# Two attention layers on eight images: the key sums' product delayed and two sums of seven given to GpSimd, layer norm taken out of ScalarE's queue, group norm between projections, opening reordered

## The chip, the core and the metric

One core of a Trainium2 chip. The metric is the device time of one execution in microseconds (us).

## The reference, cut to what matters

```python
# x: (8, 512, 32, 32) float32: 8 images (batches), 512 channels, 1024 positions
# layer 0: layer norm over channels, 8 heads of 64, projection, residual
xn = layer_norm(x_flat)
q, k, v = xn @ Wq.T + bq, xn @ Wk.T + bk, xn @ Wv.T + bv       # split in 8 heads
attn = softmax(q k^T / 8)                                        # per head, 1024 x 1024
x1 = (attn v) @ Wo.T + bo + x_flat
# layer 1: group norm (32 groups), one head of 512, projection, residual
h = group_norm(x1)
out = x1 + wp (softmax((wq h)^T (wk h) / sqrt(512)) (wv h)) + bp
```

Everything is float32.

## The kernel before

Channels lie on the partitions, four tiles of 128 x 1024 per image. Two heads (a *pair*) fill 128 partitions. A pair sees 512 query positions, so an image has 8 pairs, each worked in two *groups* of four key blocks (m = 0 to 3, then 4 to 7): 16 groups, i = 0 to 15. Softmax needs no maximum here; a check of the denominators (`junk`) guards that. The denominators come in two steps: VectorE adds up a pair's eight tiles of exponentials (the *key sums*, seven additions), and TensorE multiplies the result by ones (their *product*, `den`). To *evict* a result is to read it out of its bank of PSUM, the memory that TensorE writes, so that the bank comes free.

TensorE's order is fixed by the program. For the other engines the framework orders the queue, mostly but not always as the program gives the work: in batch 1 of this kernel GpSimd adds `x` for the mean at 640.78 us, ahead of the second pair's `o` at 657.86, which the program gives first. So orders are read from the traces below, and an edit can move more than its own lines.

```python
big  = tc.tile_pool(bufs=33)              # 128 x 1024 tiles in SBUF
ps_s = tc.tile_pool(bufs=3, space=PSUM)   # wide_psum: scores, projections, mean, variance
ps_a = tc.tile_pool(bufs=2, space=PSUM)   # bank: acc, den, group norm

class Pair:
    def scores(self, ms):                  # one group
        for m in ms:
            s = wide_psum(...)             # two matmuls into it
            p = big_tile(...)
            nc.scalar.activation(p, s, AF.Exp, scale=...)
            self.p[m] = p
            if m == 1:   self.sum = big_tile(...); nc.vector.tensor_add(self.sum, self.p[0], p)
            elif m > 1:  nc.vector.tensor_add(self.sum, self.sum, p)
    def values(self, ms): ...              # matmuls into self.acc, a bank
    def end(self):
        den = bank(...)                    # key sums' product: ones x self.sum
        o = half_tile(...);  nc.scalar.copy(o, self.acc)
        nc.vector.reciprocal(rden, den)
        check_sums(den, rden)              # junk: VectorE's last reader of den's bank
        nc.gpsimd.tensor_mul(o, o, rden)

def layer_norm_mean(b, xt):
    # x sums: three tensor_add on gpsimd; mean = ones_c x sum on TensorE
    for c in range(NC): nc.vector.tensor_sub(xt[c], xt[c], mean)
    # squares: activation(Square) on scalar, three tensor_add on gpsimd

def layer_norm_scale(b, xt, sq):
    # variance on TensorE, sqrt on scalar
    nc.vector.reciprocal(rstd, rstd)       # 128 x 1024
    for c in range(NC):
        nc.gpsimd.tensor_mul(xt[c], xt[c], rstd)
        nc.vector.tensor_scalar(xt[c], xt[c], g0, be0, ALU.mult, ALU.add)

for i, (p, ms) in enumerate(groups):       # one image
    groups[i + 1][0].scores(groups[i + 1][1])
    p.values(ms)
    if ms[-1] == NM - 1: os.append(p.end())
    if i == 3: sq = layer_norm_mean(b + 1, x_next)         # of the next image
    if i == 7: h_next = layer_norm_scale(b + 1, x_next, sq)
    if i == 9: project_out(b, 0, os[:NC], x1, stats)       # psx, then x1 = psx + bias + x
# then: two k projections of the next image, project_out of the other half,
# two k projections, group norm, layer 1
# [cuts: weight products, q/k/v projections, group norm, layer 1]
```

Of the kernel before, what the change touches and what calls it, by code (L numbers as in the profile page):

```python
# [16 lines left out]
P = 128  # L17
# [28 lines left out]
def fast_path(ctx: ExitStack, tc: tile.TileContext, x: bass.AP, vecs: dict, weights: dict, out: bass.AP,  # L46
# [46 lines left out]
    x_next = load_x(0)  # L93

# [9 lines left out]
    def load_w(pool, n):  # L104
        t = pool.tile([P, NC, C], F32, tag=f"w_{n}", name=f"w_{n}")
        nc.scalar.dma_start(out=t, in_=weights[n].rearrange("(c p) o -> p c o", p=P))
        return t

    def load_chunks(n):

        chunks = []
        for g in range(NC // 2):
            t = big_tile(f"w_{n}_{g}")
            nc.scalar.dma_start(out=t.rearrange("p (c o) -> p c o", o=C),
                                in_=weights[n][ts(g, 2 * P), :].rearrange("(c p) o -> p c o", p=P))
            chunks += [t[:, ts(k, C)] for k in range(2)]
        return chunks

# [22 lines left out]
    def weight_products():  # L141
        def natural(t, n):

            chunks = []
            for g in range(NC // 2):
                ps = wide_psum(f"pst_{n}_{g}")
                for k in range(2):
                    oc = 2 * g + k
                    for c in range(NC):
                        nc.tensor.transpose(ps[:, k * C + c * P : k * C + (c + 1) * P], t[c][:, ts(oc, P)], ident)  # L150
                r = big_tile(f"nat_{n}_{g}")
                nc.vector.tensor_copy(r, ps)
                chunks.append(r)
            return [chunks[oc // 2][:, ts(oc % 2, C)] for oc in range(NC)]

        def product(dst, lhs, rhs, n):
            for g in range(NC // 2):
                ps = wide_psum(f"psw_{n}_{g}")
                for k in range(2):
                    for oc in range(NC):  # L160
                        nc.tensor.matmul(ps[:, ts(k, C)], lhs[oc][:, ts(2 * g + k, P)], rhs(oc),
                                         start=(oc == 0), stop=(oc == NC - 1))
                nc.scalar.copy(dst[:, 2 * g : 2 * g + 2, :].rearrange("p a c -> p (a c)"), ps)

        wq, wk, wv, wp = (load_chunks(n) for n in ("q1", "k1", "v1", "p1"))
        for n in ("k0", "v0", "q0", "o0"):
            w[n] = load_w(const, n)
        nc.scalar.dma_start(out=bv0_row, in_=vecs["bv0"].rearrange("(a c) -> a c", a=1).to_broadcast((P, C)))
        nc.scalar.dma_start(out=bm_row, in_=vecs["bp1"].rearrange("(a c) -> a c", a=1).to_broadcast((P, C)))
        nq, nk = natural(wq, "q1"), natural(wk, "k1")  # L170
        product(wa, nq, lambda oc: nk[oc], "a")
        ps = bank("psu")
        for c in range(NC):
            for oc in range(NC):
                nc.tensor.matmul(ps[:, c : c + 1], nk[oc][:, ts(c, P)], vec("bq1", oc),
                                 start=(oc == 0), stop=(oc == NC - 1))
        nc.vector.tensor_copy(ua, ps[:, :NC])
        nv = natural(wv, "v1")
        product(wm, nv, lambda oc: wp[oc], "m")
        ps = bank("psb")  # L180
        for oc in range(NC):
            nc.tensor.matmul(ps, vec("bv1", oc).to_broadcast((P, P)), wp[oc],
                             start=(oc == 0), stop=(oc == NC - 1))
        nc.vector.tensor_add(bm_row, bm_row, ps)


    def layer_norm_mean(b, xt):

        t = [big_tile(f"lns_{b}_{i}") for i in range(2)]
        for i in range(2):  # L190
            nc.gpsimd.tensor_add(t[i], xt[2 * i], xt[2 * i + 1])
        nc.gpsimd.tensor_add(t[0], t[0], t[1])
        mean = wide_psum(f"mean_{b}")
        for hf in range(NH):
            nc.tensor.matmul(mean[:, ts(hf, HB)], ones_c, t[0][:, ts(hf, HB)], start=True, stop=True)
        for c in range(NC):
            nc.vector.tensor_sub(xt[c], xt[c], mean)
        sq = [big_tile(f"sq_{b}_{i}") for i in range(2)]
        nc.scalar.activation(sq[0], xt[0], AF.Square)
        for c in range(1, NC):  # L200
            nc.scalar.activation(sq[1], xt[c], AF.Square)
            nc.gpsimd.tensor_add(sq[0], sq[0], sq[1])
        return sq

    def layer_norm_scale(b, xt, sq):
# [5 lines left out]
        nc.vector.reciprocal(rstd, rstd)  # L211
        for c in range(NC):
            nc.gpsimd.tensor_mul(xt[c], xt[c], rstd)
            nc.vector.tensor_scalar(xt[c], xt[c], vec("g0", c), vec("be0", c), ALU.mult, ALU.add)  # L214
        return xt

    def group_norm(b, xt, stats):
# [10 lines left out]
        nc.vector.tensor_add(dev, dev, mv[:, :, 1])  # L228
        pv = bank(f"pv_{b}")
        nc.tensor.matmul(pv[:, :NC], grp, dev, start=True, stop=True)  # L230
        sc = small.tile([P, NC], F32, tag="gsc", name=f"gsc_{b}")
# [17 lines left out]

    def project(tag, wt, bias, ht, ocs, engine):  # L250

        res = []
        for oc in ocs:
            r = big_tile(f"{tag}_{oc}")
            ps = wide_psum(f"ps{tag}_{oc}")
            for hf in range(NH):
                for c in range(NC):
                    nc.tensor.matmul(ps[:, ts(hf, HB)], wt[:, c, ts(oc, P)], ht[c][:, ts(hf, HB)],  # L258
                                     start=(c == 0), stop=(c == NC - 1))
            if engine == "act":  # L260
                nc.scalar.activation(r, ps, AF.Identity, bias=bias(oc))  # L261
            else:
                nc.vector.tensor_scalar(r, ps, bias(oc), None, ALU.add)
            res.append(r)
# [24 lines left out]
    class Pair:  # L289
# [9 lines left out]
        def scores(self, ms):  # L299
            c, q = self.c, ts(self.hf, HB)  # L300
            for m in ms:
# [11 lines left out]
                elif m > 1:  # L313
                    nc.vector.tensor_add(self.sum, self.sum, p)  # L314

        def values(self, ms):
            if self.acc is None:
                self.acc = bank(f"acc_{self.tag}")
            for m in ms:
                for i in range(2):  # L320
                    col = self.c * P + i * D
                    nc.tensor.matmul(self.acc[i * D : (i + 1) * D, :], self.vts[m][:, col : col + D],  # L322
                                     self.p[m][:, ts(i, HB)], start=(m == 0), stop=(m == NM - 1))

        def end(self):
# [4 lines left out]
            o = half_tile(f"o_{self.tag}")  # L330
            nc.scalar.copy(o, self.acc)
# [68 lines left out]
    def head_of(b, ht):  # L400

        q = project(f"q{b}", w["q0"], lambda oc: vec("bq0", oc), ht, range(NC), "act")
        return q

    with tc.manual_schedule(engines={PE}):
        sq = layer_norm_mean(0, x_next)
        weight_products()
        ht = layer_norm_scale(0, x_next, sq)
        kt = project("k0", w["k0"], lambda oc: vec("bk0", oc), ht, range(NC), "dve")
        vts = project_v("v0", w["v0"], bv0_row, ht)  # L410
        qt = project("q0", w["q0"], lambda oc: vec("bq0", oc), ht, range(NC), "act")
        for b in range(B):
# [5 lines left out]
            os = []  # L418
            x_next = load_x(b + 1) if more else None
            groups[0][0].scores(groups[0][1])  # L420
            for i, (p, ms) in enumerate(groups):
# [3 lines left out]
                if ms[-1] == NM - 1:  # L425
                    os.append(p.end())
                if i == 3 and more:
                    sq = layer_norm_mean(b + 1, x_next)
                if i == 7 and more:
                    h_next = layer_norm_scale(b + 1, x_next, sq)  # L430
                if i == 9:
                    project_out(b, 0, os[:NC], x1, stats)
            if more:
                kn = project(f"k{b + 1}", w["k0"], lambda oc: vec("bk0", oc), h_next, (0, 1), "dve")
            project_out(b, 1, os[NC:], x1, stats)
            if more:
                kn += project(f"k{b + 1}", w["k0"], lambda oc: vec("bk0", oc), h_next, (2, 3), "act")
# [403 lines left out]
```

## Time and profile before

| | |
|---|---|
| time, median of the three first runs | 3566.05 us (3565.84 to 3566.79) |
| span of the profile | 3563.5 us |
| TensorE busy | 3344.0 us |
| first scores of heads | at 181.4 us |
| period of a batch, start of heads to start of heads | about 435 us (1 to 7), 339.3 for the last, which prepares no next image |

TensorE is the bound by its busy time. The prediction below shows these lines of the kernel before.

### The profile page before, as it was taken

How to read it: one execution, taken by the hardware profiler on the slowest of the kernel's cores; microseconds unless marked ns; L12 is line 12 of the kernel's file. 1: busy time of each engine (PE TensorE's matmuls, PEld its weight loads, DVE VectorE, ACT ScalarE, POOL GpSimd, SP SyncE). 2: the span in 40 equal slices, each digit the busy share in tenths (PEclk: the TensorE clock that was granted, in tenths of full speed). 3: DMA queues.
4: the chain of work that ended last, by engine and by line, in shares of the span. 5: the costliest groups of instructions: out<-in, count | busy, mean ns of one | idle time of the engine just before them, and what ended most of it. 6: DMA issues, size and time to landing. Idle time of an engine off the chain costs nothing.

```text
span 3563.5 us, 23451 instructions
## 1 busy us (share of the span) xinstructions
PE 3344.0 (94%) x9754; PEld 1379.6 (39%) x9754; DVE 1445.1 (41%) x1272; ACT 781.3 (22%) x819; POOL 412.5 (12%) x217
## 2 busy tenths in 40 slices
PE   5989999899997999989999899998999989999999
PEld 3433444234442344423443234433344334443343
DVE  2287111861129612285123841247412672126612
ACT  1053111521114210242102421033210441104310
POOL 1022001310013000130001200022000220010001
PEclk9999999999999999999999899999999999999999
DMA  4000001000010000100001000010000000000000
GB/s 148 0 9 16 1 0 47 9 15 0 0 48 9 15 0 6 42 12 12 0 12 36 12 12 0 12 36 12 12 0 18 30 18 6 0 24 7 17 0 25
DMA packets 34068, 60.87 MB, mean 17 GB/s; under 512 B 9120, under 2 KB 9120, under 8 KB 33952
## 3 DMA queue, kind: packets, MB, share of 16 engines
q1 hardware_dynamic: 23040, 50.34, 4.0%
q10 hardware_dynamic: 10912, 8.94, 0.8%
q8 instruction: 78, 1.28, 0.2%
q14 instruction: 38, 0.31, 0.0%
HBM read 42.49 MB, written 16.78 MB: 17 GB/s over the span
## 4 chain that ended last, share of the span: by engine, by line
PE 86%; DVE 9%; issue 2%; ACT 2%; POOL 1%; DMA 0%; DVEq 0%; ACTq 0%; SPq 0%; POOLq 0%
PE s L362 12%; PE acc L389 12%; PE s L305 10%; PE acc L322 10%; PE psqa L258 7%; PE psx L345 6%; PE psk L258 6%; PE psq L258 6%; PE psv L275 6%; PE psvm L275 6%; DVE sum L314 3%; PE den L328 2%; DVE sq L211 1%; DVE rden L333 1%; DVE x L214 1%
## 5 line engine op out<-in xcount | busy, mean ns | idle before, releaser
L308 ACT ACTIVATE p<-s 128x1024 f32<-128x1024 f32 x512 | 483.6, 1031 | 425.4 <-PE s L305 400.8
L314 DVE TENSOR_TENSOR sum<-sum,p 128x1024 f32<-128x1024 f32 x384 | 564.9, 1473 | 28.1 <-DVE sum L314 0.5
L305 PE MATMUL s<-q,k 64*128 64x512 f32 x2048 | 493.7, 620 | 69.5 <-ACT p L308 65.1
L322 PE MATMUL acc<-p,v 128*64 128x512 f32 x2048 | 472.5, 605 | 0.0
L389 PE MATMUL acc<-p,vm 128*128 128x512 f32 x1024 | 442.1, 592 | 0.0
L362 PE MATMUL s<-qa,gn 128*128 128x512 f32 x1024 | 440.8, 592 | 0.0
L305 PEld LDWEIGHTS s<-q,k 64*128 64x128 f32 x2048 | 189.0, 190 | 362.4 <-issue 194.5
L362 PEld LDWEIGHTS s<-qa,gn 128*128 128x128 f32 x1024 | 194.8, 190 | 244.6 <-issue 244.6
L389 PEld LDWEIGHTS acc<-p,vm 128*128 128x128 f32 x1024 | 194.8, 190 | 244.7 <-issue 244.7
L396 POOL TENSOR_TENSOR y<-y,x 128x512 f32<-128x512 f32 x64 | 79.6, 1264 | 1802.1 <-DVE y L395 1802.1
L258 PE MATMUL psqa<-gn,wa 128*128 128x512 f32 x512 | 239.9, 632 | 27.5 <-ACT gn L243 27.5
L322 PEld LDWEIGHTS acc<-p,v 128*64 128x64 f32 x2048 | 138.0, 139 | 327.7 <-issue 327.7
L335 POOL TENSOR_TENSOR o<-o,rden 128x512 f32<-128x512 f32 x64 | 108.2, 1691 | 1192.5 <-DVE rden L333 760.2
L258 PE MATMUL psk<-x,w_k 128*128 128x512 f32 x512 | 228.1, 604 | 15.8 <-DVE x L214 15.8
L333 DVE RECIPROCAL rden<-den 128x512 f32<-128x512 f32 x64 | 214.8, 3356 | 63.4 <-PE den L328 63.4
L345 PE MATMUL psx<-o,w_o 128*128 128x512 f32 x512 | 232.7, 614 | 2.2 <-POOL o L335 2.2
L261 ACT ACTIVATE q<-psq,vecs 128x1024 f32<-128x1024 f32 x32 | 35.6, 1113 | 848.3 <-PE psq L258 848.3
L275 PE MATMUL psv<-w_v,x 128*128 128x512 f32 x512 | 221.0, 592 | 0.0
L258 PE MATMUL psq<-x,w_q 128*128 128x512 f32 x512 | 221.0, 592 | 0.0
L275 PE MATMUL psvm<-wm,gn 128*128 128x512 f32 x512 | 221.0, 592 | 0.0
L278 DVE TENSOR_TENSOR vm<-psvm,bm_row 128x512 f32<-128x512 f32 x64 | 41.2, 686 | 427.5 <-PE psvm L275 427.5
L312 DVE TENSOR_TENSOR sum<-p,p 128x1024 f32<-128x1024 f32 x64 | 93.4, 1459 | 285.9 <-ACT p L308 285.9
(97 smaller groups left out, 1884.7 us busy)
## 6 DMA issues: line engine op xcount, KB each, us to landing
x<-in_x_dram SPq DMA_DIRECT2D x32, 512.0 KB, 5.8
xr<-in_x_dram SPq DMA_DIRECT2D x64, 256.0 KB, 2.8
out_dram<-y SPq DMA_DIRECT2D x64, 256.0 KB, 2.0
w_k<-in_L_conv_Wk_dram ACTq DMA_DIRECT2D x1, 1024.0 KB, 5.6
w_v<-in_L_conv_Wv_dram ACTq DMA_DIRECT2D x1, 1024.0 KB, 7.9
w_q<-in_L_conv_Wq_dram ACTq DMA_DIRECT2D x1, 1024.0 KB, 10.1
w_o<-in_L_conv_Wo_dram ACTq DMA_DIRECT2D x1, 1024.0 KB, 12.2
w_q<-in_L_conv_wq_dram ACTq DMA_DIRECT2D x2, 512.0 KB, 3.9
```

The source lines that it names most:

```text
L258: nc.tensor.matmul(ps[:, ts(hf, HB)], wt[:, c, ts(oc, P)], ht[c][:, ts(hf, HB)], start=(c == 0), stop=(c == NC - 1))
L275: nc.tensor.matmul(ps[:, ts(k, C)], ht[c][:, ts(2 * g + k, P)], wt[:, c, :], start=(c == 0), stop=(c == NC - 1))
L305: nc.tensor.matmul(s[:, ts(i, HB)], self.kt[c][r, ts(m, P)], self.qt[c][r, q], start=True, stop=True)
L308: nc.scalar.activation(p, s, AF.Exp, scale=1.0 / float(D) ** 0.5)
L312: nc.vector.tensor_add(self.sum, self.p[0], p)
L314: nc.vector.tensor_add(self.sum, self.sum, p)
L322: nc.tensor.matmul(self.acc[i * D : (i + 1) * D, :], self.vts[m][:, col : col + D], self.p[m][:, ts(i, HB)], start=(m == 0), stop=(m == NM ...
L333: nc.vector.reciprocal(rden, den)
L335: nc.gpsimd.tensor_mul(o, o, rden)
L345: nc.tensor.matmul(ps[:, ts(k, HB)], w["o0"][:, c, ts(oc, P)], ot[c], start=(c == 0), stop=(c == NC - 1))
L362: nc.tensor.matmul(s[:, ts(hf, HB)], ht[c][:, ts(m, P)], qt[c][:, ts(hf, HB)], start=(c == 0), stop=(c == NC - 1))
L389: nc.tensor.matmul(acc[:, ts(hf, HB)], vts[m][:, ts(oc, P)], pt[m][:, ts(hf, HB)], start=(m == 0), stop=(m == NM - 1))
```

## The change

Its intent is to clear the four places where TensorE stands still in the kernel before.

```diff
 # heads: two of the seven sums of a pair start on GpSimd ("half sums", tile two)
-                elif m > 1:
+                elif m in (3, 5):
+                    two = big_tile(f"two_{self.tag}_{m}")
+                    nc.gpsimd.tensor_add(two, self.p[m - 1], p)
+                    nc.vector.tensor_add(self.sum, self.sum, two)
+                elif m > 5:
                     nc.vector.tensor_add(self.sum, self.sum, p)
 # the copy of acc moves from end() to the end of values(); end() is called a group later
-                if ms[-1] == NM - 1:
-                    os.append(p.end())
-                if i == 3 and more:
-                    sq = layer_norm_mean(b + 1, x_next)
-                if i == 7 and more:
-                    h_next = layer_norm_scale(b + 1, x_next, sq)
-                if i == 9:
+                if ended is not None:
+                    os.append(ended.end())
+                ended = p if ms[-1] == NM - 1 else None
+                if i == 5 and more:
+                    sq = layer_norm_mean(b + 1, x_next, False)
+                if i == 10:
+                    if more:
+                        h_next = layer_norm_scale(b + 1, x_next, sq)
                     project_out(b, 0, os[:NC], x1, stats)
 # layer norm: squares on GpSimd (first image: ScalarE, with all sums on VectorE)
+            if first:
+                nc.scalar.activation(to, xt[c], AF.Square)
+            else:
+                nc.gpsimd.tensor_mul(to, xt[c], xt[c])
 # layer norm: scale and bias
-        nc.vector.reciprocal(rstd, rstd)
+        for hf in range(NH):
+            nc.vector.reciprocal(rstd[:, ts(hf, HB)], rstd[:, ts(hf, HB)])
         for c in range(NC):
-            nc.gpsimd.tensor_mul(xt[c], xt[c], rstd)
-            nc.vector.tensor_scalar(xt[c], xt[c], vec("g0", c), vec("be0", c), ALU.mult, ALU.add)
+            nc.vector.scalar_tensor_tensor(xt[c], xt[c], vec("g0", c), rstd, ALU.mult, ALU.mult)
+            nc.gpsimd.tensor_scalar(xt[c], xt[c], vec("be0", c), 1.0, ALU.add, ALU.mult)
 # group norm: halves of the last k projection behind its two small products
+        meanwhile(0)
         pv = bank(f"pv_{b}")
         nc.tensor.matmul(pv[:, :NC], grp, dev, start=True, stop=True)
+        meanwhile(1)
 # [cut: opening: weights of q1 load first, all weights on one queue, the first mean
 #  and the first scaling between the weight products; k evictions on ScalarE]
```

## The prediction

> **What bounds the kernel now.** I first read the page for the share of the engines and for the chain that ended last.
>
> ```profile
> PE 3344.0 (94%) x9754; PEld 1379.6 (39%) x9754; DVE 1445.1 (41%) x1272; ACT 781.3 (22%) x819; POOL 412.5 (12%) x217
> ...
> PE 86%; DVE 9%; issue 2%; ACT 2%; POOL 1%; DMA 0%; DVEq 0%; ACTq 0%; SPq 0%; POOLq 0%
> ```
>
> TensorE is the bound, and the change removes none of its matmuls. All it can win is TensorE's idle time (3563.5 - 3344 = 219.5 us) and slow matmuls beside it. I next asked who TensorE waits for, then laid batch 1 (616.4 to 1052.5 us) out in windows, whose columns are length, then busy time of each engine.
>
> ```profile
> PE s L305 <- ACT p L308: 65.1, 15, 8.0
> PE den L328 <- DVE sum L314: 57.3, 7, 9.4
> PE psqa L258 <- ACT gn L243: 27.5, 8, 3.6
> ```
>
> ```profile
> 0.00:181.40 181.40, 138.93 (x353) 66.63 (x353) 38.99 (x32) 15.29 (x14) 25.61 (x19) 0.93 0.22 73
> 616.40:649.50 33.10, 33.10 (x151) 12.09 (x152) 26.30 (x18) 20.41 (x22) 10.68 (x4) 1.00 0.00 0
> 649.50:670.00 20.50, 12.25 (x44) 3.75 (x40) 20.08 (x13) 8.46 (x9) 8.38 (x5) 0.83 0.00 1
> ...
> 693.40:721.50 28.10, 18.55 (x69) 5.76 (x68) 25.47 (x14) 11.92 (x12) 12.84 (x5) 0.87 0.06 19
> ...
> 823.00:829.00 6.00, 1.59 (x6) 0.94 (x5) 2.84 (x10) 4.92 (x5) 0.00 (x0) 0.82 0.00 0
> 829.00:1052.50 223.50, 223.50 (x518) 98.68 (x516) 31.82 (x36) 17.36 (x17) 9.94 (x8) 0.99 0.05 19
> ```
>
> The holes sit in three places of a batch and in the opening; elsewhere TensorE is full. In two of the three, VectorE is 98% and 91% busy. The chain of waits through the first hole tells how a busy VectorE stops TensorE:
>
> ```profile
> 648.49 3.31 DVE sum L312
> ...
> 654.37 3.35 DVE rden L333
> 657.72 0.07 DVE x L197
> ...
> 660.63 0.04 ACT sq L201
> ...
> 661.59 1.01 ACT p L308
> ...
> 662.65 3.78 PE s L305 x8
> ```
>
> ScalarE's next exponentials stand in its queue behind layer norm's squares, these wait for the subtraction on VectorE, and that stands behind key sums (3.3 us instead of 1.2) and a reciprocal. TensorE has no free score bank until the exponentials run.
>
> For sizes I use a floor: an undisturbed score stage of layer 1 takes 54.93 us for 128 recorded matmuls, 0.429 us each; heads' matmuls run two at a time, so 0.215. Time above it in batch 1, start to start: scores after the mean 13.68 for 16, 10.25 over; scores after the variance 3.2 and values 1.2 over; the second values 11.38 for 16, 7.95 over, as the key sums' product waits for the last sum; that product and the output projection behind it 1.05 and 2.4 over (0.7 to 2.4 by batch); group norm 6.2 over. Sum about 31.5 us. Some 5 us of 0.05 to 0.2 at every change of stage will stay.
>
> **What the Trainium skill says.** "SBUF — State Buffer", section "SBUF: two separate sides": a GpSimd operation and a VectorE one with two SBUF inputs or in a 2-port mode exclude each other for the whole instruction. The trace agrees: an undisturbed sum takes 1.225 us (the median), and beside GpSimd's additions 3.2 to 3.4, about 2.35 + 1. "GPSIMD Engine Reference", section "Elementwise — side-by-side cycle accounting": a two-input addition is 1.96 times as long as on VectorE; here 2.35 against 1.225, a ratio of 1.92. The same page, "Engine selection": one-input work on GpSimd is about line rate; no trace of the kernel before has such an instruction, so I estimate 1.1 us for 1024 elements from the page. "TensorE: Matmul & The Clock Gate", Part 1: an idle window of about 3.4 us halves the clock until as long a busy one has passed. The trace agrees: after the first hole eight score matmuls took 3.78 us, twice the rate above, so a hole costs up to 2 us beyond its length.
>
> **The change, part by part.**
>
> ```profile
> L314 DVE TENSOR_TENSOR sum<-sum,p 128x1024 f32<-128x1024 f32 x384 | 564.9, 1473 | 28.1 <-DVE sum L314 0.5
> L333 DVE RECIPROCAL rden<-den 128x512 f32<-128x512 f32 x64 | 214.8, 3356 | 63.4 <-PE den L328 63.4
> L213 POOL TENSOR_TENSOR x<-x,sq 128x1024 f32<-128x1024 f32 x32 | 91.1, 2877 | 97.4 <-DVE sq L211 97.4
> L214 DVE TENSOR_SCALAR x<-x,vecs 128x1024 f32<-128x1024 f32 x32 | 58.7, 1877 | 18.1 <-POOL x L213 18.1
> ```
>
> *Sums.* A pair of heads takes TensorE 15.2 us. VectorE's share was 7 x 1.225 + 3.36 + 0.69 + 0.08 = 12.7 us, before any collision. Two sums of seven pass to GpSimd: VectorE 10.3, GpSimd 2 x 2.35 + 1.27 = 6.0. Of the 2.45 us saved, collisions can take back most (a sum that meets an addition waits up to 2.1), so the balance is a small gain in an ordinary pair. The real gain is time: the product stands one group (7.2 us) later, and the measured wait for the last sum was 7.7. The copy of the values leaves with the last values, so the bank is not held.
>
> *Layer norm off ScalarE's queue.* The squares (4 x 1.06 on ScalarE) become 4 x 2.35 on GpSimd. No exponential stands behind a late subtraction any more: the 10.25 goes unless TensorE waits for the mean's sums. From 649.5 (mean) to 693.3 (variance) was 44 us with its stall; the new distance is five groups, 5 x 7.15 + 2.5 x 0.95 = 38 us. GpSimd's work in it: 4 squares and 3 sums, 7 x 2.35 = 16.5; five pair sums, 11.8; 2.5 multiplications, 3.2; total 31.5. With 12.5 sums of VectorE on the same ports at about 1 us: 44 us in 38. Some must slip, and the delayed product can absorb about 7 us. I put 4 us per batch on this. The scaling becomes 4 x 1.23 on VectorE and about 4 x 1.1 on GpSimd instead of 4 x 2.88 and 4 x 1.88, the reciprocal is split into halves of 3.3 so that a sum can come between, and 13.7 us of output projection follows the variance, which hides the square root and its table loads (1.28 each). Of 13 to 15 us I leave 1.
>
> *Group norm.*
>
> ```profile
> 824.28 1.28 ACT L233 ACT_TABLE_LOAD   x1
> 825.58 0.26 ACT L233 ACTIVATE gsc<-pv,eps 128x4 f32<-128x4 f32 x1
> ```
>
> Two halves of a k projection, 8 x 0.429 = 3.4 us each, come behind the two small products. The first covers 0.9 us of VectorE, the second the path of 0.3 + 0.27 + 0.8 + 1.25 = 2.6. The table load no longer stands behind the last projection's eviction on ScalarE. Of 6.2 us 1 stays.
>
> *Opening.* TensorE's floor to the first head's scores is about 131 us and it takes 181.4: it waits 16.7 for the mean, then for weights queued behind others, then 14.5 for the scaling. Afterwards: first weights and identity at about 6.5; transposes 4; x lands by about 13, VectorE's sums to 15.5, mean to 19; transposes of k 4; half a product 7, variance 2, the other half 7; transposes of v 3.4, product 13.7: 57 us. The scaling, from 33 on, takes 1.3 + 1.1 + 6.6 + 4.9 + 1.1 = 15, so it is done by 48. Then 3 x 27.5 and 7.1 of vectors: 147. Saving 34; I take 32 for a slower clock.
>
> *Sum.* Removed: 7 x 31.5 = 220 (the last batch has neither layer norm nor spare projections). Left or new: 7 x (mean 1.5 + ports 4 + variance 1 + group norm 1) = 52. Opening 32. 3566 - 220 + 52 - 32 = 3366; I say **3365 us**.
>
> **Rivals.** *GpSimd and the shared ports become the bound.* GpSimd's queue is in order; if the seven layer norm instructions run ahead of the pair sums, a pair sum comes up to 23 us late (7 x 3.3), less than 14 us of which the delay covers: 9 us per batch in place of my 4, or some 12 with the clock; 3400 to 3425. For it: 44 us of port work in 38. Against it: GpSimd is 12% busy over the run, and stretches beside the window have about 2 us to spare per group. *Buffers.* Sums, halves of sums and the next x live longer in the same 33 tiles; an exponential without a tile stops TensorE as before: 3 to 6 us per batch, 3385 to 3410. No line of the profile shows such a wait now. *Everything hides:* only the 5 us of changes of stage stay, 3315. *The opening waits for transfers*, now on one queue: 10 us worse at most, as four weights of 1 MB landed about 2.7 us apart (issued 0.5 us apart, 5.6, 7.9, 10.1 and 12.2 from issue to landing).
>
> **Range and chances.** Everything hidden and the first rival with some buffers bound it: 3320 to 3425 holds it 8 times in 10. A gain of 2% means 3494.7; the opening and group norm alone give 67, so both other holes would have to stay almost whole. Chances: 0.94 faster, 0.05 within 2%, 0.01 slower.
>
> **What would show it.** The waits of scores for exponentials and of the product for the last sum should fall from 65 and 57 us to a few; group norm's 27.5 to under 8; the first scores come near 147 us instead of 181; VectorE's sums of the heads are 64 x 5 = 320 instead of 448, GpSimd busy some 412 + 128 x 2.35 + 7 x (4 x 2.35 + 4 x 1.1 - 11.4) = 730 us. The batch period falls from 436 to about 412. It is wrong if TensorE's waits move to the variance or the product behind late GpSimd work, if sums beside GpSimd average over 1.8 us, or if the exponentials wait for tiles.

## The result, and the profile after

Ratios here are the mean time of one kernel's fast runs over that of the kernel before in the same rounds, so not quite the ratio of the medians quoted.

| | before | after |
|---|---|---|
| median of four runs, us | 3566.14 (3565.84 to 3566.79) | 3532.88 (3529.51 to 3534.0) |
| ratio, 95% interval | | 0.9905 (0.9888 to 0.9922) |
| mean granted clock | 0.969 | 0.971 |
| first scores of heads, us | 181.4 | 151.3 |
| period of a batch, us | 434 to 436 | 434 to 435 |

The changed kernel is 0.95% faster. The last two rows of the table tell where that is from: the opening gave 30.1 us of the 33, and a batch takes as long as before. The prediction had 3365 us and a period of 412.

The busy times and the shares of the chain that ended last, of the changed kernel:

```profile
PE 3333.7 (94%) x9754; PEld 1371.1 (39%) x9754; DVE 1285.9 (36%) x1145; ACT 769.2 (22%) x804; POOL 732.3 (21%) x367
...
PE 78%; DVE 10%; POOL 8%; issue 3%; ACT 1%; DMA 0%; ACTq 0%; DVEq 0%; POOLq 0%; SPq 0%
```

The work moved as planned: VectorE lost 159 us of busy time, and GpSimd has 732 us, where 730 were predicted. But GpSimd's share of the chain rose from 1% to 8%. TensorE's waits (columns: who waits for whom, us in all, times, longest) say at which place:

```profile
PE mean L180 <- POOL lns L177: 70.8, 7, 10.1
PE s L302 <- DVE x L355: 44.3, 14, 6.3
PE acc L323 <- DVE junk L283: 36.2, 7, 5.9
...
PE psqa L243 <- DVE gn L236: 8.7, 7, 1.2
...
PE s L302 <- ACT p L305: 2.4, 6, 0.8
```

The waits that the prediction named inside a batch are gone: 2.4 us are left of the 65.1 for exponentials, none of the 57.3 of the product for the last sum, 8.7 (and 2.4 in the last batch, which has no spare projection) of group norm's 27.5. The three upper rows are new (for the mean the kernel before had 18.7 us, but 16.7 of them in the opening), and come 7 or 14 times: once or twice in every batch that prepares a next image. The windows of batch 1 (columns: stretch; length; busy time and instructions of TensorE, weight loads, VectorE, ScalarE, GpSimd; clock, DMA share, GB/s) place them:

```profile
631.50:650.00 18.50, 8.38 (x24) 2.74 (x24) 7.69 (x6) 1.99 (x3) 12.47 (x5) 0.67 0.00 0
650.00:682.00 32.00, 27.05 (x108) 8.89 (x106) 22.22 (x13) 12.23 (x13) 25.45 (x11) 0.87 0.03 9
...
712.00:724.20 12.20, 5.90 (x17) 1.83 (x16) 11.39 (x13) 2.77 (x3) 7.45 (x4) 0.72 0.01 2
724.20:1020.60 296.40, 295.16 (x758) 127.02 (x756) 65.12 (x77) 38.83 (x40) 24.36 (x15) 1.00 0.05 18
```

TensorE is full in the long last stretch. In the first it is 45% busy at a clock of 0.67, and GpSimd is the busiest engine (67%); in the second GpSimd is 80% busy; in the third VectorE is 93% busy. Each has a cause of its own.

**First hole, the mean.** TensorE asks for the mean's sum at 635.2 and gets it at 645.4. GpSimd's timeline (start, length, instruction):

```profile
632.76 1.27 POOL L338 TENSOR_TENSOR o<-o,rden 128x512 f32<-128x512 f32 x1 [7.27 <-DVE rden L336]
633.99 3.33 POOL L312 TENSOR_TENSOR two<-p,p 128x1024 f32<-128x1024 f32 x1
637.28 5.62 POOL L176 TENSOR_TENSOR lns<-x,x 128x1024 f32<-128x1024 f32 x2
642.97 2.34 POOL L177 TENSOR_TENSOR lns<-lns,lns 128x1024 f32<-128x1024 f32 x1
```

The image was there in time (the kernel before added it two groups earlier). Its three sums stand in GpSimd's queue behind the product of the heads' output with `rden`, which waited 7.3 us for VectorE's reciprocal, and behind a half sum. They are given to the queue at i == 5, in the same step in which TensorE asks for their result. The kernel before did that too, at i == 3, but there no half sum stood on GpSimd and the sums ran ahead of the second pair's `o`:

```profile
640.78 6.63 POOL L191 TENSOR_TENSOR lns<-x,x 128x1024 f32<-128x1024 f32 x2
647.49 3.22 POOL L192 TENSOR_TENSOR lns<-lns,lns 128x1024 f32<-128x1024 f32 x1
657.86 1.26 POOL L335 TENSOR_TENSOR o<-o,rden 128x512 f32<-128x512 f32 x1 [7.16 <-DVE rden L333]
```

They ended at 650.7, and TensorE waited 0.3 us.

**Second hole, a bank.** TensorE's values wait 4.8 us from 669.8, for a bank that the check `junk` frees:

```profile
674.60 5.69 PE L323 MATMUL acc<-p,v 128*64 128x512 f32 x16 [4.83 <-DVE junk L283]
```

VectorE up to there:

```profile
661.05 3.37 DVE L313 TENSOR_TENSOR sum<-sum,two 128x1024 f32<-128x1024 f32 x1 [7.19 <-POOL two L312]
664.52 6.02 DVE L315 TENSOR_TENSOR sum<-sum,p 128x1024 f32<-128x1024 f32 x2
670.46 3.35 DVE L336 RECIPROCAL rden<-den 128x512 f32<-128x512 f32 x1
673.84 0.69 DVE L283 SCALAR_TENSOR_TENSOR junk<-den,rden 128x512 f32<-128x512 f32 x1
```

VectorE did nothing for 7.2 us, because the half sum stood on GpSimd behind two squares, their sum and a third square (650.5 to 658.7). Its next three sums took 3.4 and 3.0 each instead of 1.225, as they met GpSimd's next instructions (two additions and a square, 661.0 to 669.4) on the shared ports. Then the reciprocal and the check came too late for the bank.

**Third hole, the evictions of the output projection.** VectorE when the scores of the next group want a score bank:

```profile
705.03 6.56 DVE L200 RECIPROCAL sq<-sq 128x512 f32<-128x512 f32 x2
711.51 0.65 DVE L355 SCALAR_TENSOR_TENSOR x<-psx,vecs,xr 128x512 f32<-128x512 f32 x1
712.08 5.64 DVE L202 SCALAR_TENSOR_TENSOR x<-x,vecs,sq 128x1024 f32<-128x1024 f32 x4
717.64 0.68 DVE L356 BATCH_NORM_STATS2 stats<-x 128x6 f32<-128x512 f32 x1
718.24 1.39 DVE L355 SCALAR_TENSOR_TENSOR x<-psx,vecs,xr 128x512 f32<-128x512 f32 x2
```

The projection's results lie in two of the three score banks. Their evictions (L355) stand behind layer norm's reciprocals (6.6 us) and, but for the first, behind its scaling (5.6 us) too, so TensorE's scores wait from 713.1 to 719.0:

```profile
719.02 2.08 PE L302 MATMUL s<-q,k 64*128 64x512 f32 x4 [5.88 <-DVE x L355]
```

By the floor of the prediction (each matmul at its undisturbed pace), batch 1 still lies 36.5 us above it, after 38.7 before: 14.2 around the mean (10.3 of waiting, 3.9 of slow clock behind it), 7.2 around the bank, 8.8 around the projection, 1.5 at group norm, and 4.8 in changes of stage.

### The profile page after: what moved, and what is told of

It is laid out like the page before. It is cut to its first block, busy times and chain, and to the rows that moved or that the text cites. A ratio compares the mean times of both kernels' runs of the same rounds, so it can differ in the third digit from the quotient of the medians.

```text
span 3531.5 us, 23399 instructions
## 1 busy us (share of the span) xinstructions
PE 3333.7 (94%) x9754; PEld 1371.1 (39%) x9754; DVE 1285.9 (36%) x1145; ACT 769.2 (22%) x804; POOL 732.3 (21%) x367
## 4 chain that ended last, share of the span: by engine, by line
PE 78%; DVE 10%; POOL 8%; issue 3%; ACT 1%; DMA 0%; ACTq 0%; DVEq 0%; POOLq 0%; SPq 0%
PE s L365 12%; PE acc L392 12%; PE s L302 8%; PE acc L323 8%; PE psk L243 6%; PE psq L243 6%; PE psvm L272 6%; PE psv L272 6%; PE psqa L243 6%; PE psx L348 3%; POOL two L312 3%; DVE rden L336 2%; DVE sum L313 2%; DVE sum L315 1%; POOL sq L188 1%
## 5 line engine op out<-in xcount | busy, mean ns | idle before, releaser
L302 PE MATMUL s<-q,k 64*128 64x512 f32 x2048 | 497.5, 624 | 46.8 <-DVE x L355 44.3
L323 PE MATMUL acc<-p,v 128*64 128x512 f32 x2048 | 481.8, 614 | 36.2 <-DVE junk L283 36.2
L312 POOL TENSOR_TENSOR two<-p,p 128x1024 f32<-128x1024 f32 x128 | 342.6, 2684 | 470.7 <-ACT p L305 470.7
L313 DVE TENSOR_TENSOR sum<-sum,two 128x1024 f32<-128x1024 f32 x128 | 233.7, 1826 | 331.0 <-POOL two L312 328.7
L243 PE MATMUL psqa<-gn,wa 128*128 128x512 f32 x512 | 225.2, 598 | 11.1 <-DVE gn L236 8.7
L348 PE MATMUL psx<-o,w_o 128*128 128x512 f32 x512 | 224.5, 596 | 2.2 <-POOL o L338 2.2
L309 DVE TENSOR_TENSOR sum<-p,p 128x1024 f32<-128x1024 f32 x64 | 101.5, 1586 | 236.2 <-ACT p L305 235.8
```

The lines of the kernel that those rows point to most:

```text
L243: nc.tensor.matmul(ps[:, ts(hf, HB)], wt[:, c, ts(oc, P)], ht[c][:, ts(hf, HB)], start=(c == 0), stop=(c == NC - 1))
L302: nc.tensor.matmul(s[:, ts(i, HB)], self.kt[c][r, ts(m, P)], self.qt[c][r, q], start=True, stop=True)
L312: nc.gpsimd.tensor_add(two, self.p[m - 1], p)
L313: nc.vector.tensor_add(self.sum, self.sum, two)
L323: nc.tensor.matmul(self.acc[i * D : (i + 1) * D, :], self.vts[m][:, col : col + D], self.p[m][:, ts(i, HB)], start=(m == 0), stop=(m == NM ...
L348: nc.tensor.matmul(ps[:, ts(k, HB)], w["o0"][:, c, ts(oc, P)], ot[c], start=(c == 0), stop=(c == NC - 1))
```

## The experiments

The theory after reading this: *the half sums on GpSimd are a loss, and the three holes come from orders within queues that the change brought about* ("queues" in the expectations). Rivals: the shared ports as such (everything GpSimd does slows VectorE; "ports"), and the output's loop (VectorE's reciprocal, then GpSimd's product `o`, then GpSimd's half sum, then VectorE again). All runs gave correct results and were timed in three rounds, the last two in five.

| kernel | median, us | ratio to before, 95% interval |
|---|---|---|
| changed kernel | 3532.9 | 0.9905 (0.9888 to 0.9922) |
| 1 opening and group norm alone | 3502.5 | 0.9825 (0.9809 to 0.9842) |
| 2 changed, all sums on VectorE | 3458.3 | 0.9696 (0.9680 to 0.9713) |
| 3 changed, x sums early | 3494.6 | 0.9801 (0.9784 to 0.9817) |
| 4 changed, `o` on VectorE | 3517.3 | 0.9865 (0.9849 to 0.9882) |
| 5 changed, projection first | 3503.5 | 0.9825 (0.9809 to 0.9842) |
| 6 changed, sums of two pairs on VectorE | 3477.2 | 0.9755 (0.9738 to 0.9771) |
| 7 changed, squares on ScalarE | 3500.2 | 0.9817 (0.9801 to 0.9834) |
| 8 changed, with 2, 3 and 5 together | 3357.6 | 0.9420 (0.9404 to 0.9435) |
| 9 as 8, half sums on GpSimd in all pairs | 3454.1 | 0.9680 (0.9664 to 0.9696) |
| 10 as 8, half sums on GpSimd in six pairs | 3425.9 | 0.9604 (0.9588 to 0.9620) |
| 11 as 8, product at once | 3402.4 | 0.9534 (0.9518 to 0.9550) |
| 12 as 8, squares on ScalarE | 3382.0 | 0.9480 (0.9464 to 0.9496) |
| 13 as 10, `o` on VectorE | 3421.6 | 0.9596 (0.9580 to 0.9612) |
| 14 as 9, `o` on VectorE | 3454.4 | 0.9687 (0.9671 to 0.9703) |
| 15 as 8, half sums in the four clear pairs | 3389.5 | 0.9510 (0.9496 to 0.9524) |
| 16 as 15, `o` on VectorE | 3384.9 | 0.9494 (0.9481 to 0.9507) |

### 1. The two sure parts alone

```diff
 # the changed kernel, with heads, sums, layer norm and the order of groups put back:
-                elif m in (3, 5): ...            # half sums
+                elif m > 1:
+                    nc.vector.tensor_add(self.sum, self.sum, p)
-                if i == 5 and more:              # mean;  scale at i == 10
+                if i == 3 and more:              # mean;  scale at i == 7, end() at once
```

> The opening and the group norm of the change alone; heads, sums and layer norm as before. Both theories (queues: the new waits come from GpSimd's and VectorE's in-order queues standing behind each other; ports: GpSimd and VectorE have more work on their shared SBUF ports than time) say the same: the opening gives 30 us (first scores at 151 instead of 181), group norm 7 x 5 = 36, the waits of scores for exponentials (65) and of the product for the last sum (57) stay: 3500 us, some 33 less than the changed kernel, so the moved sums and layer norm would have cost more than they gave.

Measured 3502.5 us. The opening and group norm alone beat the whole change by 30 us. The first scores come at 148.2 us in this run, so 33.2 of the 63.6 us are the opening's. About 30, 4.3 a batch, are left for group norm's placing (with the k evictions on ScalarE), where 5.2 were predicted. So the rest of the change, sums, product and layer norm, is a loss of 30 us as it stands. The two old waits are all there, at 65.5 (product) and 65.4 us (exponentials).

### 2. All sums on VectorE

```diff
-                elif m in (3, 5):
-                    two = big_tile(f"two_{self.tag}_{m}")
-                    nc.gpsimd.tensor_add(two, self.p[m - 1], p)
-                    nc.vector.tensor_add(self.sum, self.sum, two)
-                elif m > 5:
+                elif m > 1:
                     nc.vector.tensor_add(self.sum, self.sum, p)
```

> The changed kernel with all seven sums of a pair on VectorE again, one by one. Queues and ports both: GpSimd no longer holds anything that a sum waits for, so the wait for the mean (71), for the bank behind the check (36) and much of that for the output projection's bank (44) fall: 3533 - 100 = about 3430. A third theory, that VectorE at 12.7 us a pair plus 16 of layer norm becomes the bound: the product waits for the sums again and the time is 3500 or more.

Measured 3458.3 us, 75 us less than the changed kernel, where 100 were expected. What the prediction had as a small gain in an ordinary pair is the dearest part of the change. The wait for the bank is gone (0.2 us); those for the mean (53.2) and the projection (37.0) stay, so they have causes beside the half sums. Collisions on the ports are not where VectorE's time went in the changed kernel: its 320 additions of key sums on VectorE take 516 us, the 448 here take 644, so VectorE did keep 2.0 us a pair of the 2.45. What it lost was waiting, 328.7 us, for half sums.

### 3. The x sums early

```diff
+                if i == 2 and more:
+                    xs = x_sums(b + 1, x_next, False)      # the three GpSimd additions
                 if i == 5 and more:
-                    sq = layer_norm_mean(b + 1, x_next, False)
+                    sq = layer_norm_mean(b + 1, x_next, False, xs)
```

> The changed kernel with layer norm's three sums of x given to GpSimd three groups earlier, nothing else moved. Queues: the wait for the mean falls from 71 us to under 10 and the time by 60 to 80, to about 3460. Ports: the same work collides elsewhere, the waits behind the check and the output projection grow by what the mean loses, and the time stays within 15 of 3533.

Measured 3494.6 us: only 38 us for a wait of 70.8. TensorE's waits in this kernel:

```profile
PE acc L328 <- DVE junk L288: 43.4, 7, 6.5
PE s L307 <- DVE x L360: 43.0, 14, 6.3
PE s L307 <- DVE x L188: 16.4, 7, 2.6
PE s L307 <- ACT p L310: 13.5, 22, 2.4
```

The mean's wait is gone. In its place scores wait 16.4 us for the subtraction that frees the mean's bank, the bank behind the check costs 7.2 us more and the exponentials 11.1 more. Together 34.7 us come back, and 70.8 - 34.7 = 36 is about what was won. A hole removed alone passes half of its gain on to the next late thing, here VectorE behind the half sums.

### 4. The output's product on VectorE

```diff
-            nc.gpsimd.tensor_mul(o, o, rden)
+            nc.vector.tensor_mul(o, o, rden)
```

> The changed kernel with the heads' multiplication by the inverse on VectorE (0.7 us) instead of GpSimd (1.27), so that no instruction of GpSimd in the heads waits for VectorE's reciprocal any more. Queues: the loop of 15.3 us (product, halves of sums, sums, reciprocal, product) is cut; the mean's wait falls by 6 of 10 us a batch and the two later waits by half or more: about 3440 to 3470. Ports: 1.27 us less of some 11 a pair, so 10 to 20 us at most: 3515.

Measured 3517.3 us, 16 less, which is what the ports had been expected to give. The wait for the mean is still 66.2 us and that for the bank 39.0. So the mean's sums are not late because of the product that waits for VectorE, and breaking the loop is not the cure here.

### 5. The output projection ahead of the scaling

```diff
                 if i == 10:
+                    project_out(b, 0, os[:NC], x1, stats)
                     if more:
                         h_next = layer_norm_scale(b + 1, x_next, sq)
-                    project_out(b, 0, os[:NC], x1, stats)
```

> The changed kernel with the output projection's half given before layer norm's variance and scaling, so that on VectorE the projection's evictions stand ahead of the two half reciprocals and the scaling. If the third hole (scores after the projection, 8.8 us a batch, 44 us counted as waits) comes only from this order: that wait falls to near nothing and the time by 50 to 60, to about 3475. If VectorE is simply late there whatever stands first (the ports' backlog): the wait passes to the key sums' product or to the bank behind the check, and less than 20 us is won.

Measured 3503.5 us, 29 less. The wait of 44.3 us for the evictions is gone, and that for the bank rose from 36.2 to 55.2 us, now twice a batch. That lies between the two expectations: again a part is passed on.

### 6. The sums of the two pairs beside the squares on VectorE

```diff
+            self.beside = b + 1 < B and (hf, c) in ((0, NC - 1), (1, 0))
...
+                elif self.beside and m > 1:
+                    nc.vector.tensor_add(self.sum, self.sum, p)
                 elif m in (3, 5):
```

> The changed kernel with the sums of only the two pairs beside layer norm's squares (the last of the first half, the first of the second half) on VectorE; the other six pairs keep two sums on GpSimd. If the sums on GpSimd cost only where they meet layer norm there: the wait for the bank behind the check (36) is gone and the time is that with all sums on VectorE, 3458, within 10. If the sums on GpSimd cost in every pair: about a quarter of the 75 us, some 3515.

Measured 3477.2 us: 56 of the 75 us of experiment 2, for two pairs of eight. Neither expectation holds. Most of the loss sits where half sums stand among layer norm's work in GpSimd's queue, but not all of it.

### 7. Squares back on ScalarE

```diff
-            if first:
-                nc.scalar.activation(to, xt[c], AF.Square)
-            else:
-                nc.gpsimd.tensor_mul(to, xt[c], xt[c])
+            nc.scalar.activation(to, xt[c], AF.Square)
```

> The changed kernel with the squares on ScalarE again (4 x 1.06 us a batch), the additions of the squares still on GpSimd. Ports and GpSimd's queue: GpSimd is 9.4 us shorter a batch beside the pairs, the bank's wait behind the check falls from 36 to under 10. But exponentials stand behind subtractions again: if these are late the wait for exponentials comes back with up to 65 us; if they are in time because VectorE has fewer sums, little. I expect 3500, with the wait for the mean unchanged at 71.

Measured 3500.2 us, 33 less than the changed kernel. The bank's wait is gone, with the squares that the half sum stood behind; the mean's stays at 70.8. Taken by itself, this would make the squares' move look like a mistake. Experiment 12 shows the opposite in the cured kernel.

### 8. The three cures together

Experiments 2, 3 and 5 in one kernel.

> All three cures together: sums on VectorE, the sums of x three groups earlier, the projection ahead of the scaling; late product, squares on GpSimd, group norm and opening stay. If the holes were caused by these three placements: 3458 less 53 and 14 for the mean and less 50 for the projection: 3340 to 3360. If VectorE at 12.7 us a pair plus 25 of layer norm and projection in some 138 becomes the bound, waits of the product for the sums come back and it is 3400 or more.

Measured 3357.6 us (3357.2 to 3360.9), 5.8% under the kernel before and the fastest of all. Singly the cures gave 75 + 38 + 29 = 142 us, together 175. The busy times and the waits of this kernel:

```profile
PE 3292.0 (98%) x9754; PEld 1358.1 (40%) x9754; DVE 1414.4 (42%) x1273; ACT 767.2 (23%) x804; POOL 431.4 (13%) x239
```

```profile
PE s L307 <- ACT p L310: 11.1, 15, 1.2
PE mean L185 <- DVE lns L176: 9.6, 1, 9.6
PE psqa L248 <- DVE gn L241: 8.7, 7, 1.2
...
PE acc L324 <- DVE junk L288: 4.1, 9, 1.2
```

VectorE is busier by 128 us than in the changed kernel, and the kernel is 175 us faster: VectorE's load was not what the changed kernel suffered from, but when its results came. A batch takes 409.6 us, with 12.1 us over the floor; TensorE is busy 98% of the time. The one wait for the mean left is that of the opening.

### 9 and 10. Half sums back into the cured kernel

```diff
 # 9: in all eight pairs; 10: in all but the two pairs beside the squares
-                elif m > 1:
+                elif m in (3, 5):
+                    two = big_tile(f"two_{self.tag}_{m}")
+                    nc.gpsimd.tensor_add(two, self.p[m - 1], p)
+                    nc.vector.tensor_add(self.sum, self.sum, two)
+                elif m > 5:
```

> The changed kernel with the two cures of order (sums of x earlier, projection first) and the two half sums of a pair still on GpSimd. If the half sums are the cause of their own hole (VectorE idle for a half sum that stands behind layer norm's squares in GpSimd's queue): the wait for the bank behind the check stays at 40 us or more and the time is 3533 less 38 and 29, about 3465, some 100 above the kernel with all three cures. If the third cure is worth only what was left over by the other two: within 30 of 3358.

> All cures, but only the two pairs beside layer norm's squares have their sums on VectorE, the other six keep two half sums on GpSimd. If half sums on GpSimd are harmless away from layer norm: within 10 of 3358, perhaps below it, as VectorE has 2 x 1.2 us less a pair. If they cost in ordinary pairs too, what separated the two kernels with sums on VectorE everywhere and beside layer norm alone, 19 us, comes back: about 3377.

Measured 3454.1 us for all pairs, 96 over experiment 8, with the wait for the bank up from 4.1 to 62.6 us, as expected of half sums that make a hole of their own. With six pairs 3425.9 us, still 68 over. Both expectations of experiment 10 fell: the squares are not the only thing that hurts. Per pair of the seven batches it is 96 / 56 = 1.7 and 68 / 42 = 1.6 us.

A pair is *late* here when VectorE comes to it behind TensorE, so that it finds all exponentials ready. What happens then shows best side by side. VectorE of experiment 8, from one reciprocal to the next:

```profile
640.92 3.35 DVE L337 RECIPROCAL rden<-den 128x512 f32<-128x512 f32 x1
...
646.86 7.87 DVE L316 TENSOR_TENSOR sum<-sum,p 128x1024 f32<-128x1024 f32 x6
654.65 3.35 DVE L337 RECIPROCAL rden<-den 128x512 f32<-128x512 f32 x1
```

GpSimd of experiment 10, from one output product to the next:

```profile
658.05 1.27 POOL L346 TENSOR_TENSOR o<-o,rden 128x512 f32<-128x512 f32 x1 [11.13 <-issue]
659.28 5.65 POOL L320 TENSOR_TENSOR two<-p,p 128x1024 f32<-128x1024 f32 x2
673.35 1.27 POOL L346 TENSOR_TENSOR o<-o,rden 128x512 f32<-128x512 f32 x1 [8.42 <-DVE rden L344]
```

With VectorE alone a late pair takes 13.7 us. TensorE takes 15.2 for a pair, so each pair regains 1.5 us. With the half sums it takes 15.3: the output product waits for the reciprocal, the half sums stand behind the product, VectorE's sums wait for the half sums and collide with them. So a pair that is late stays late, although VectorE has less work in it. The changed kernel has the same 15.3 (output products at 673.89 and 689.16).

### 11. The product at once

```diff
-                if ended is not None:
-                    os.append(ended.end())
-                ended = p if ms[-1] == NM - 1 else None
+                if ms[-1] == NM - 1:
+                    os.append(p.end())
```

> All three cures, but the product of the key sums right behind the pair's last values, as before the change. If the later product is what buys VectorE its time in layer norm's stretch: the wait of the product for the last sum comes back with 5 to 8 us a batch or more, 3358 + 50 = about 3410. If the cures made it needless: within 10 of 3358.

Measured 3402.4 us: the later product is worth 45 us in the cured kernel, with 35.4 us of the product's wait for the last sum back in the trace.

### 12. Squares on ScalarE in the cured kernel

The edit of experiment 7, in the kernel of experiment 8.

> All three cures, with layer norm's squares on ScalarE again. If exponentials behind late subtractions still stop TensorE: a hole of about 5 us a batch after the mean, 3358 + 35 = about 3390. If the subtractions come in time now, GpSimd's four squares fewer make no difference or help: within 10 of 3358.

Measured 3382.0 us: squares off ScalarE are worth 24 us here, mostly as scores wait 28.2 us for exponentials instead of 11.1. In the changed kernel the same edit won 33. So the sign of this part depends on the rest of the kernel. Half sums beside the squares in GpSimd's queue are the likely reason, but the two kernels differ in all three cures, so that is not shown alone.

### 13 and 14. Is it the output's loop?

The loop of experiment 10 is broken by the edit of experiment 4: `o` on VectorE, with half sums in six pairs (13) and in all (14).

> The kernel with all cures of order and half sums on GpSimd for six pairs of eight (3426 us), with the heads' multiplication by the inverse on VectorE. There, while VectorE is late, a pair takes 15.3 us from one multiplication to the next (658.05 to 673.35), no less than TensorE's 15.25, so it never catches up; with all sums on VectorE it takes 13.7. Loop (GpSimd's next half sum stands behind a multiplication that waits for VectorE's reciprocal, and VectorE's next sum waits for the half sum): with the multiplication on VectorE the cycle is 0.69 + 0.69 + 5 x 1.33 + 3.35 = 11.4 and some collisions, below 13, and the time 3360 or less. Ports (half sum and sum shut each other out, 3.3 us each): the cycle only loses 1.3, to 14, and the time stays above 3400.

> The same with half sums on GpSimd in all pairs (3454 us). The hole where a half sum stands behind layer norm's squares (about 10 us a batch, waits for the bank behind the check) stays in the pair beside them in either theory; loop: VectorE then catches up and the later waits go, about 3420; ports: 3440 to 3454.

VectorE of experiment 13, from one output product to the next, with the sums of a pair between them whose half sums have a free queue:

```profile
609.76 0.86 DVE L346 TENSOR_TENSOR o<-o,rden 128x512 f32<-128x512 f32 x1
...
620.99 0.69 DVE L346 TENSOR_TENSOR o<-o,rden 128x512 f32<-128x512 f32 x1
```

The late pair now takes 11.2 us, less than with all sums on VectorE, as the loop theory said. Yet the time is 3421.6, only 4 us less, and in experiment 14 nothing is won at all (3454.4). So the loop makes the late cycle long, but it is not the main cause of the loss. VectorE's waits in experiment 13 show what is left:

```profile
DVE sum L321 <- POOL two L320: 144.7, 38, 7.0
```

The longest, 7.0 us each, are half sums that stand behind the three x sums of layer norm; others stand behind its bias.

### 15 and 16. Half sums only in pairs with nothing of layer norm ahead of them

```diff
+            self.beside = b + 1 < B and (hf, c) in ((0, 1), (0, 3), (1, 0), (1, 2))
 # 15: o on GpSimd, 16: o on VectorE
```

> All cures of order; half sums on GpSimd only in the four pairs of eight ahead of which nothing of layer norm stands in GpSimd's queue (not beside the sums of x, the squares or the bias); multiplication on GpSimd. If half sums cost because they stand behind layer norm's instructions there: within 10 of 3358. If the loop with the multiplication costs in each pair as well: half of the 68 us between 3426 and 3358 at least stays, about 3385 to 3400.

> The same with the multiplication on VectorE, which cut the cycle of a late pair from 15.3 to some 11 to 13 us in the run before. Standing behind layer norm as the only cost: within 10 of 3358, or up to 15 below it, for VectorE then has less to do in four pairs. If even here half sums cost (ports): 3375 or more.

Measured 3389.5 and 3384.9 us, 32 and 27 over experiment 8: with half sums in four pairs with a free queue ahead the kernel still loses, 32 / 28 = 1.1 us a pair, in place of 1.6 to 1.7. Keeping clear of layer norm brings back the larger part, and no placing tried here made half sums on GpSimd pay. But these pairs do not leave layer norm clear: the half sums of the first pair stand ahead of the x sums in GpSimd's queue, so that these start 9.7 us after the first scores in batch 1 and later ones (1.5 us before them in experiment 8), beside VectorE's additions, which then take up to 3.3 us each. Collisions took back all of the work that was saved: VectorE adds key sums for 646 us in experiment 15 and for 643 in experiment 8, with 72 additions fewer. How the last 27 to 32 us divide between these collisions and VectorE's waiting for half sums (107.8 us in experiment 15, 65.9 in 16) stays open.

In all six kernels from 9 on with half sums the loss reaches TensorE mostly as the wait for the bank behind the check: 62.6, 44.5, 51.9, 88.4, 27.7 and 24.8 us (experiments 9, 10 and 13 to 16) against 4.1 in experiment 8. No run moved the check, so whether half sums would pay if the bank came free earlier is not tested. In experiments 6, 10, 13, 15 and 16 the last batch kept its half sums in all pairs; that batch takes 337 to 342 us in every kernel.

## Why the prediction was wrong

**Right: what the change removes.** Every wait named went: exponentials 65.1 to 2.4, product 57.3 to none, first scores at 151.3 instead of 147. Group norm's 6.2 over the floor became 1.5 where 1 was left. Its timeline shows the two small products between the halves of the projection:

```profile
790.25 0.28 PE L212 MATMUL pm<-mv,grp 128*128 128x4 f32 x2
790.39 3.68 PE L243 MATMUL psk<-x,w_k 128*128 128x512 f32 x8
793.90 0.28 PE L220 MATMUL pv<-gdev,grp 128*128 128x4 f32 x2
794.04 3.68 PE L243 MATMUL psk<-x,w_k 128*128 128x512 f32 x8
```

**Wrong: "Left or new: 7 x (mean 1.5 + ports 4 + variance 1 + group norm 1) = 52".** In the order of these terms the trace has 14.2, 7.2, 8.8 and 1.5, which is 31.7 a batch instead of 7.5. The difference, 7 x 24.2 = 169 us, added to the 3366 of the sum gives 3535; measured were 3533. Batch 1 stands for all seven here, so the agreement to 2 us is partly luck, but the miss is in this line, and in three of its terms:

- *Mean 1.5, measured 14.2.* I asked whether TensorE waits for the mean's sums and put 1.5 us on it, without asking where these stand in GpSimd's queue. They are 8 us of work, given at the moment when they are needed, behind a half sum that the change put there. Three groups earlier the wait is gone (experiment 3). The clock was under-sized too: "up to 2 us beyond its length" was 3.9 behind this hole, with a granted clock of 0.50 from 645.3 to 650.8 us and full speed only from 652.5.
- *Ports 4, measured 7.2.* My sum of "44 us in 38" said that work would slip, and that the delayed product could absorb 7 us. The product did absorb it. But the lateness went on to the check behind the product, which holds a bank that the next values need; I had named no bank of PSUM among the buffers.
- *Variance 1, measured 8.8.* "13.7 us of output projection follows the variance, which hides the square root" is true of TensorE. But the projection's evictions follow the scaling in VectorE's queue as well, and they hold two of three score banks. I followed one engine's order and not the other's. With the projection first this wait is gone (experiment 5).

**Wrong beneath it: "the balance is a small gain in an ordinary pair".** The 2.45 us of VectorE's work saved a pair, less collisions, were the wrong quantity. VectorE did lose the work, 2.0 us a pair. What counts for TensorE is when the last sum of a pair comes, and that now has a trip to GpSimd's queue in it: VectorE waited 328.7 us for half sums in the changed kernel, and a late pair needs 15.3 us instead of 13.7 (this alone is not the cost: cut to 11.2 us in experiment 13 it won 4 us). Measured, half sums cost 75 us in the changed kernel and 96 in the cured one. They also make the other terms worse: the bank's wait is theirs and the squares' together (experiments 2 and 7 each remove it).

**The signs.** Of the three signs of being wrong that the prediction named, the first came true in kind: TensorE's waits moved to late GpSimd work, though to the mean, the bank and the evictions and not to the variance or the product. VectorE's additions of key sums average 1.61 us, those that take a half sum 1.83, about the 1.8 named. The exponentials did not wait for tiles.

**The rivals.** The first, GpSimd and its ports as the bound, pointed to the right engine: half sums and layer norm's work behind each other in one queue. It gave 9 to 12 us per batch for that in place of 4, 3400 to 3425 in all, and so fell short by over 100 us, because it counted the mean and the evictions as hidden. The second rival, exponentials without a tile, reached TensorE for at most the 2.4 us above. The transfers did not either: the first weights' wait is 5.6 us in all.

**What was worth what.** The chances (0.94 for a gain of over 2%) rested on the old holes not staying whole. They went, as said; that the change would make new ones as large was left out. Experiment 8 keeps the opening, the later product, the squares, the scaling and group norm's placing, and with 409.6 us a batch and 3357.6 in all is where the prediction had put the change (412 and 3365). That does not confirm the prediction's sum, as this kernel has no half sums and two orders that the prediction did not have. In it the later product is worth 45 us and the squares 24; opening and group norm give 63.6 by experiment 1. That is 133 of the 208 us below the kernel before; the other 75 were not separated, since parts that cover the same wait do not add up.

## What to carry to other kernels

Before giving part of a chain to an idle engine, write down what stands ahead of it in that engine's queue, and what it will stand ahead of. Compare how long one round of the chain takes when it is late with the pace of the bounding engine: here 15.3 us against 15.2 regained nothing, 13.7 did. A short round is not enough, though: 11.2 us with `o` on VectorE won only 4 us. Follow the frees as well as the data: an eviction that gives a bank back belongs ahead of long work in its queue (29 us in experiment 5), and work needed at a step should be given to its engine some steps earlier (38 us in experiment 3). When a change of many parts moves little, time its parts alone and together, as one bad part can turn the worth of a good one (squares on GpSimd lost 33 us in the changed kernel and won 24 in the cured one).

## What the Trainium skill lacked or had wrong

- "GPSIMD Engine Reference", section "Engine selection", sends an elementwise addition of two tiles to VectorE, as about twice as long on GpSimd. The runs agree with the advice, but the length alone does not explain the cost here: half sums cost 75 to 96 us in all although GpSimd is 21% busy and VectorE 36%. What the pages state is about length and ports; I found none that says what a chain loses that goes from VectorE to GpSimd and back through two in-order queues: 328.7 us of VectorE's waiting, 15.3 us for a late pair instead of 13.7.
- The same section has one-input work at about line rate. The bias on GpSimd (128 x 1024) took 1.12 us at its shortest, as estimated from it, but 1.60 in the median and 3.20 at most, next to VectorE's scaling with two SBUF inputs (1.27 to 2.06 us). That fits the exclusion that "SBUF — State Buffer", section "Who interferes with whom", states; the rate alone is too low an estimate for such a place.
- "GPSIMD Engine Reference", section "Elementwise — side-by-side cycle accounting", gives one figure for two-input work. A square written as the product of a tile with itself took 1.89 us undisturbed, an addition of two tiles 2.35; the page does not tell these apart.
- "VectorE: DVE Perf Modes", section "First, the fixed hardware budget", says that the reciprocal is an iterated divide, and gives no time. It took 3.35 us for 128 x 512, against 1.225 for a sum of twice the elements, and it stands in every late pair shown above.
